# A fused attention and neighbour kernel: batch 0's distances in float32r parts, 45 unread products ahead, last rows in two banks, another order

## Chip, cores and metric

The kernel runs on one core of a Trainium2 chip. The metric is the device time of one execution in microseconds (us), the median over runs. Lower is better. Engines are named as in the profile: PE is the matrix engine (PEld its weight loads), DVE the vector engine, ACT the scalar engine, POOL the general engine, SP the engine that issues DMAs.

## What is computed

Four stages on x of shape 4 x 256 x 512 (batch, rows, features), with a context of 64 x 512 per batch:

```
# stage 0: a mixture of 8 low-rank updates
w   = softmax(x @ router_W.T + router_b)              # 8 weights per row
a   = x @ sum_over_batches(ctx).T                     # 64 values per row
x   = nan_to_num(x + 0.5 * sum_n w_n * (a @ lora_B[n].T))
# stage 1: attention of 32 heads of 16 over the 64 context rows, with a mask
q, k, v = x @ Wq.T + bq, ctx @ Wk.T + bk, ctx @ Wv.T + bv
x   = layernorm(x + (softmax(mask(q k / 4)) v) @ Wo.T + bo) * ln_g + ln_b
# stages 2 and 3 (the same twice): 4 blocks each over the 8 nearest of 512 points
d2  = sq[:, None] + sq[None, :] - 2 * ctx.T @ ctx     # ctx[b]: 512 points in 64 dimensions
idx = top 8 of -d2                                    # per point, same for both stages
for i in range(4):
    p = leaky_relu(x)
    x = (W[i] @ p + sum over 8 neighbours of W[i] @ p[:, idx]) / 9 + x
```

The points lie in the feature axis: 512 points, each with 64 context rows as coordinates. The matrix W[i] is 256 x 256 and the same for the centre and the neighbours, so that a block is one product with W[i] and one with a 0/1 matrix of 512 x 512 (`nbr`), which has a one for the point itself and for its 8 nearest.

## The kernel before

**How the order comes about.** The program doesn't write its instructions in the order of execution. Each step is handed to a planner (`Plan.add`) with its engine, an assumed cost, what it reads and writes, and for some steps a second engine that could do it. `Plan.emit` then walks over modelled time: of all steps that are ready it takes, per engine, the one with the least rank among those that could start first, and emits it. Rank is the batch's due time (`DEADLINES`, line 32, one number per batch) less the length of the longest chain behind the step. `RATES` (line 46) are assumed DMA rates, `LAG` what a DMA transpose takes to land. Engines execute their queue in the emitted order, so the assumed costs decide the order but not the durations.

**Loads.** All loads are issued by SP in the order of the lines 300 to 324, over eight lanes: `load_points(b)` is batch b's context as 64 x 512 (`raw`), `ctxT` the transposed context of all batches, `load_k(o)` a quarter of WkT, `load_xT`, `load_x`, `load_w` the rest. Batch 0's context goes to a tile of its own, `cxx0`, twice: once to the partitions 0 to 63 and once to 64 to 127.

**Start.** DVE sets `ones`; PE then makes `WARM` = 20 products of 128 x 128 from it whose result nobody reads (line 333). `lora_a` sums the context over batches into `rw`. `keys` makes kT from ctxT and WkT (line 720), and ACT or DVE copy it out with bias into `kbd` (lines 736, 748).

**Per batch.** `mixture(b)`: routing products (line 421), the softmax of the 8 weights, `z` (line 449), its transpose (`turn`, line 467 on PE for batches 0 and 1, a DMA transpose for 2 and 3), the update products (line 523, with lora_BT). `values` (line 780), `queries` (line 818), `attention` (lines 848, 859, 945, 965), layer norm. `nearest(b)`: distances, then the best 8 of each row (lines 646, 649), a 0/1 matrix `near` (656, 665), a DMA transpose (675), and a copy into `nbr` (689). `block(b, i)`, i = 0 to 7: `wp` = W[i] p (line 1021), split into an upper float32r part and the rest (lines 1034, 1037), then the product of both with `nbr` (line 1052) and the update of x (line 1068).

**Distances.** The nearest need exact products. For batches 1 to 3, `scores(b)` splits the context into its float32r value and the rest: `chl` holds value and rest above each other in 128 partitions, `clh` the rest and the value, `csq` the squares in the same two parts. Three float32r products of 128 rows make one bank of 128 x 512 distances (lines 627, 628, 629). The splits take four ACT steps of 64 x 512 (lines 607 to 610) and three POOL steps (line 615). For batch 0, `scores_first` makes the cross product as float32 from `cxx0` instead, 64 rows deep, two banks at a time in the two halves of the array (line 585), and adds the squares with one float32r product per bank (line 598).

**End.** The last batch's last block ends with `last`: the second half of the neighbour sum for rows 128 to 255 is made in two column halves of 256 (line 1090), both in the bank that holds the first half of the sum; each half has its own update (line 1107) and its own store (line 1116).

Of the kernel before, what the change touches and what calls it, by code (L numbers as in the profile page):

```python
# [8 lines left out]
F32 = mybir.dt.float32  # L9
BF16 = mybir.dt.bfloat16  # L10
F32R = mybir.dt.float32r
# [20 lines left out]
DEADLINES = (0.0, 35.0, 60.0, 67.0)  # L32
# [9 lines left out]
WARM = 20  # L42
# [22 lines left out]
class Plan:  # L65
# [39 lines left out]
    def emit(self, deadline):  # L105
# [16 lines left out]
        while ready:  # L122
# [45 lines left out]
            op.end += op.lag  # L168
# [13 lines left out]
def xattn_seq_kernel(ctx: ExitStack, tc: tile.TileContext, a: dict, out: bass.AP):  # L182
# [23 lines left out]
    def make(kind, place, name):  # L206
# [15 lines left out]


    csq0 = keep.tile([128, H], F32R, name="csq0")
    cxx0 = keep.tile([128, H], F32, name="cxx0")
    chl = {b: keep.tile([128, H], F32R, name=f"chl{b}") for b in range(1, B)}
    clh = {b: keep.tile([128, H], F32R, name=f"clh{b}") for b in range(1, B)}
# [5 lines left out]
        ["csq0", "cxx0", "chl1", "clh1"],  # L233
# [60 lines left out]
    def load_points(b):  # L294
        if b:
            load(raw[b], 0.13, lambda: raw[b].tile[0:64], a["ctx"][b])
        else:
            load("cxx", 0.13, lambda: cxx0[0:64], a["ctx"][0])

    load_points(0)  # L300
    load("cxx2", 0.13, lambda: cxx0[64:128], a["ctx"][0])
    load("small", 0.05, lambda: consts, a["small"])
    load("ctxT", 0.5, lambda: ctxT.rearrange("p c b v -> p (c b v)"), a["ctxT"])
    load_k(0)
    load_k(2)
# [3 lines left out]
    load_k(3)  # L309
    load_w("lora_BT")  # L310
    load_points(3)
    load_points(2)
    load_x(0)
    load_w("WvT")
    load_x(1)
    load("rows1", 0.5, lambda: rows1, a["rows1"].partition_broadcast(128))
# [3 lines left out]
    load_xT(1)  # L320
    load_xT(2)
# [9 lines left out]
        2.2,  # L331
# [176 lines left out]
    def mix(b, l, zb):  # L508
# [44 lines left out]
        act(0.63, lambda: A_.activation(odd.tile, v, AF.Identity, bias=zero, scale=0.0), (key, "zero"), (odd,))  # L553
# [14 lines left out]
    def scores_first(b, dist):  # L568

        sq = Buf("half", "sq0")  # L570
        act(0.6, lambda: A_.activation(sq.tile[0:64], cxx0[0:64], AF.Square), ("cxx",), (sq,))
        act(0.6, lambda: A_.copy(csq0[0:64], sq.tile[0:64]), (sq,), ("csq",))
        dve(
            0.69,
            lambda: V_.tensor_tensor(csq0[64:128], sq.tile[0:64], csq0[0:64].bitcast(F32), ALU.subtract),
            (sq, "csq"),
            ("csq2",),
            port=True,
        )
        for k in range(2):  # L580

            def cross(k=k):
                for j in (2 * k, 2 * k + 1):
                    r = slice(64 * (j % 2), 64 * (j % 2) + 64)
                    T_.matmul(
                        dist[j].tile,
                        lhsT=cxx0[r, bass.ts(j, 128)],
                        rhs=cxx0[r],
                        start=True,
                        stop=False,  # L590
                        tile_position=(64 * (j % 2), 0),
                    )

            pe(2.1, cross, ("cxx", "cxx2"), (dist[2 * k], dist[2 * k + 1], ("d2", b, 4 + k)))
            for j in (2 * k, 2 * k + 1):
                pe(
                    0.36,
                    lambda j=j: T_.matmul(dist[j].tile, lhsT=mhalf_r, rhs=csq0, start=False, stop=True),
                    ("csq", "csq2", "mhalf_r"),
                    (dist[j], ("d2", b, j)),  # L600
                )

    def scores(b, dist):
# [8 lines left out]
        def rest(out_, whole, upper, ins, key):  # L612
            pool(
                1.3,
                lambda: G_.tensor_tensor(out_(), whole.tile[0:64], upper().bitcast(F32), ALU.subtract),
                (whole, *ins),
                (key,),
            )
# [19 lines left out]
    def nearest(b):  # L638
# [46 lines left out]
        for k in range(H // 128):  # L685
# [10 lines left out]
            if b > 1:  # L696
                gone = [("d2", i, j) for i in (2 * b - 4, 2 * b - 3) for j in range(4 if i else 6)]
# [488 lines left out]
```

## Time and profile before

| | |
|---|---|
| median of 3 runs | 385.94 us (385.63 to 387.9) |
| the profiled execution | 386.5 us, its span 384.8 us |
| PE, PEld busy | 378.7, 291.5 us |
| DVE, ACT, POOL busy | 240.0, 191.3, 110.3 us |
| costliest lines on PE | L1021 120.1 us, L1052 110.3 and 99.6 us |
| loads | 25.46 MB moved by the hardware queue, HBM read 12.87 MB |

The span is the time from the first to the last instruction of the program in the profiled execution; the execution's own time has 1.7 us around it. Matrix products are pipelined: the duration of one includes its latency, so consecutive ones overlap in the profile, and what counts in a stream is the distance from start to start. A number after a line or group such as "x16" is how many instructions of the kind are merged in it; a float32 product counts twice. What stands in brackets is the idle time of the engine ahead of it and what ended it.

### The profile page before, as it was taken

The page shows a single profiled execution, that of the slowest core. Times are in us where ns is not written, and L with a number is a line of the kernel's source. Part 1 is how long each engine was busy: PE and PEld are TensorE (multiplying, and loading weights), DVE is VectorE, ACT ScalarE, POOL GpSimd, SP SyncE. Part 2 cuts the span into 40 slices and gives each one's busy share as a digit, 9 for nine tenths or more (in the row PEclk, how much of TensorE's full clock was granted, in tenths as well). Part 3 has the DMA queues.
Part 4 walks back from the last instruction along what each step waited for, and adds up shares of the span by engine and source line. Part 5 has one row for each costly group of instructions (what it writes and reads, how often), then busy time and mean ns, then how long its engine had stood idle before and what let it go on. Part 6 is the DMA issues. An engine that isn't in the chain of part 4 may idle for free.

```text
span 384.8 us, 5507 instructions
## 1 busy us (share of the span) xinstructions
PE 378.7 (98%) x2120; PEld 291.5 (76%) x2120; DVE 240.0 (62%) x445; ACT 191.3 (50%) x296; POOL 110.3 (29%) x122
## 2 busy tenths in 40 slices
PE   8999999999999999999999999999999999999996
PEld 5848747668887666887867767888888888888885
DVE  1779599995992876955966726535435435435433
ACT  2672755759688769775757722322222221222220
POOL 5483307676356426542054430400000000000000
PEclk9999999999999999999999999999999999999999
DMA  6999500162155305215014610000000001000002
GB/s 201 343 407 348 112 15 1 29 136 42 28 111 112 68 0 110 56 20 90 3 27 89 103 55 2 0 0 2 1 0 2 1 0 56 0 0 2 0 0 111
DMA packets 47386, 25.81 MB, mean 67 GB/s; under 512 B 43200, under 2 KB 43584, under 8 KB 46720
## 3 DMA queue, kind: packets, MB, share of 16 engines
q1 hardware_dynamic: 47360, 25.46, 26.6%
q8 instruction: 17, 0.28, 0.3%
q14 instruction: 9, 0.07, 0.1%
HBM read 12.87 MB, written 2.10 MB: 39 GB/s over the span
## 4 chain that ended last, share of the span: by engine, by line
PE 84%; DVE 9%; DMA 2%; SPq 2%; ACT 2%; issue 1%; DVEq 0%
PE blk L1052 31%; PE wp L1021 29%; PE q L818 7%; PE o L965 5%; PE upd L523 4%; DMA raw<-in_ctx 2%; SPq L273 2%; PE avT L945 2%; PE v L780 1%; PE route L421 1%; PE s L859 1%; DVE rest L649 1%; DVE den L900 1%; DVE s L891 1%; DVE mx L885 1%; DVE top L646 1%
## 5 line engine op out<-in xcount | busy, mean ns | idle before, releaser
L1021 PE MATMUL wp<-fT,p 128*128 128x256 f32 x512 | 120.1, 380 | 0.0
L1052 PE MATMUL blk<-nbr,wph 128*128 128x512 f32 x254 | 110.3, 434 | 0.0
L1021 PEld LDWEIGHTS wp<-fT,p 128*128 128x128 f32 x512 | 96.6, 189 | 17.9 <-issue 2.5
L1052 PE MATMUL blk<-nbr,wpl 128*128 128x512 f32 x254 | 99.6, 392 | 0.0
L1068 DVE SCALAR_TENSOR_TENSOR x<-blk,x 128x512 f32<-128x512 f32 x63 | 42.9, 683 | 69.5 <-PE blk L1052 69.5
L1034 ACT CAST wph<-wp 128x512 fp32r<-128x512 f32 x64 | 37.3, 583 | 94.9 <-PE wp L1021 94.6
L1037 DVE TENSOR_TENSOR wpl<-wp,wph 128x512 fp32r<-128x512 f32 x64 | 43.8, 685 | 37.7 <-ACT wph L1034 37.7
L1052 PEld LDWEIGHTS blk<-nbr,wph 128*128 128x128 f32 x254 | 47.8, 188 | 11.8 <-issue 1.1
L1052 PEld LDWEIGHTS blk<-nbr,wpl 128*128 128x128 f32 x254 | 47.8, 188 | 10.2 <-DVE wpl L1037 0.5
L922 POOL TENSOR_TENSOR s<-s,rden 128x512 f32<-128x512 f32 x32 | 32.6, 1052 | 53.4 <-DVE rden L912 53.4
L1004 ACT ACTIVATE p<-x 128x512 f32<-128x512 f32 x38 | 24.0, 630 | 30.4 <-DVE x L1068 26.6
L477 ACT COPY pT_a<-s 128x1024 uint16<-128x1024 uint16 x24 | 24.6, 1044 | 10.8 <-POOL s L922 6.5
L965 PE MATMUL o<-WoT,avTs 128*128 128x512 f32 x64 | 29.7, 596 | 0.0
L523 PE MATMUL upd<-lora_BT,zTs 128*128 128x512 f32 x64 | 28.8, 597 | 0.8 <-ACT zTs L471 0.8
L818 PE MATMUL q<-x1T,WqT 128*128 128x256 f32 x128 | 29.1, 382 | 0.1
L818 PEld LDWEIGHTS q<-x1T,WqT 128*128 128x128 f32 x128 | 24.0, 190 | 4.0 <-ACT x1T L471 0.6
L523 PEld LDWEIGHTS upd<-lora_BT,zTs 128*128 128x128 f32 x64 | 11.9, 190 | 14.9 <-issue 13.2
L897 ACT ACTIVATE s<-s 128x512 f32<-128x512 f32 x32 | 18.6, 626 | 7.4 <-DVE s L891 7.4
L885 DVE TENSOR_REDUCE mx<-s 128x8 f32<-128x512 f32 x32 | 20.2, 679 | 2.2 <-PE s L859 2.2
L965 PEld LDWEIGHTS o<-WoT,avTs 128*128 128x128 f32 x64 | 11.9, 189 | 11.1 <-issue 10.3
L891 DVE TENSOR_TENSOR s<-s,mx 128x512 f32<-128x512 f32 x32 | 20.2, 678 | 0.0
L900 DVE TENSOR_REDUCE den<-s 128x8 f32<-128x512 f32 x32 | 20.0, 673 | 0.1
(124 smaller groups left out, 415.5 us busy)
## 6 DMA issues: line engine op xcount, KB each, us to landing
xT<-in_xT SPq DMA_DIRECT2D x4, 512.0 KB, 9.7
x<-in_x SPq DMA_DIRECT2D x4, 512.0 KB, 11.2
out<-x SPq DMA_DIRECT2D x7, 256.0 KB, 2.0
WkT<-in_WkT SPq DMA_DIRECT2D x4, 256.0 KB, 6.5
lora_BT<-in_lora_BT SPq DMA_DIRECT2D x1, 1024.0 KB, 9.4
WvT<-in_WvT SPq DMA_DIRECT2D x1, 1024.0 KB, 11.1
rows<-in_rows SPq DMA_DIRECT2D x2, 512.0 KB, 12.3
WoT<-in_WoT SPq DMA_DIRECT2D x1, 1024.0 KB, 11.7
```

The lines of the kernel that those rows point to most:

```text
L477: lambda: A_.copy(apart.tile.bitcast(U16).rearrange("p (t n) -> p t n", t=2), src().bitcast(U16).rearrange("p (n t) -> p t n", t=2),),
L523: T_.matmul(ps2.tile, lhsT=zT.tile[:, bass.ts(c, 128)], rhs=w["lora_BT"][:, c, :], start=(c == 0), stop=(c == NC - 1),)
L818: T_.matmul(ps.tile[:, 0:S], lhsT=w["WqT"][:, c, bass.ts(o, 128)], rhs=x1T[b].tile[:, c, :], start=(c == 0), stop=(c == NC - 1),)
L885: lambda mx=mx, ps=ps: V_.tensor_reduce(mx.tile[:, 0:HPC], heads(ps), AX.X, ALU.max),
L891: lambda mx=mx, ps=ps, s=s: V_.tensor_tensor(heads(s), heads(ps), mx.tile[:, 0:HPC].unsqueeze(2).to_broadcast([128, HPC, V]), ALU.subtract),
L922: lambda s=s, g=g: G_.tensor_tensor(heads(s), heads(s), rden.tile[:, bass.ts(g, HPC)].unsqueeze(2).to_broadcast([128, HPC, V]), ALU.mult,),
L965: T_.matmul(po.tile, lhsT=avT.tile[:, bass.ts(c, 128)], rhs=w["WoT"][:, c, :], start=(c == 0), stop=(c == NC - 1),)
L1021: T_.matmul(ps.tile[:, bass.ts(k, S)], lhsT=p.tile[:, c, bass.ts(2 * m2 + k, 128)], rhs=wi[:, c, :], start=(c == 0), stop=(c == NL - 1),)
L1034: act(0.59, lambda ps=ps, hi=hi: A_.copy(hi.tile, ps.tile), (ps,), (hi,))
L1037: lambda ps=ps, hi=hi, lo=lo: V_.tensor_tensor(lo.tile, ps.tile, hi.tile.bitcast(F32), ALU.subtract),
L1052: T_.matmul(pb[o].tile, lhsT=part.tile[:, bass.ds(m % 2 * S + o * 128, 128)], rhs=nbr[b, m], start=(m == 0 and k == 0), stop=(m == H // 12 ...
L1068: lambda o=o: V_.scalar_tensor_tensor(pt[:, o], pb[o].tile, 1.0 / (KNN + 1.0), pt[:, o], ALU.mult, ALU.add),
```

## The change

1. Batch 0's distances go through `scores` like those of the other batches; `scores_first`, `csq0` and `cxx0` are gone. Batch 0's context is loaded once, into `raw`, and gets `chl` and `clh` tiles of its own. Its three subtractions are done by DVE, those of the other batches still by POOL.
2. `WARM` goes from 20 to 45, its assumed cost from 2.2 to 5.0.
3. `last` makes each column half in a bank of its own, both halves of the neighbour sum in it, so that the first half of the sum is split into columns too.
4. The order of the loads changes: ctxT is issued second, the small constants after WkT's first quarter, x of batch 0 before lora_BT, WvT before the context of batches 2 and 3, rows1 after xT1.
5. The planner's numbers change: the due times, two assumed ACT costs, and the end of a DMA transpose, which is now never ahead of the last load.

```diff
-DEADLINES = (0.0, 35.0, 60.0, 67.0)
+DEADLINES = (0.0, 33.0, 58.0, 65.0)
...
-WARM = 20
+WARM = 45
...
-            op.end += op.lag
+            if op.lag:
+                op.end = max(op.end, self.landed[-1]) + op.lag
...
-    csq0 = keep.tile([128, H], F32R, name="csq0")
-    cxx0 = keep.tile([128, H], F32, name="cxx0")
-    chl = {b: keep.tile([128, H], F32R, name=f"chl{b}") for b in range(1, B)}
-    clh = {b: keep.tile([128, H], F32R, name=f"clh{b}") for b in range(1, B)}
+    chl = {b: keep.tile([128, H], F32R, name=f"chl{b}") for b in range(B)}
+    clh = {b: keep.tile([128, H], F32R, name=f"clh{b}") for b in range(B)}
...
-        ["csq0", "cxx0", "chl1", "clh1"],
+        ["chl0", "clh0", "chl1", "clh1"],
...
     load_points(0)
-    load("cxx2", 0.13, lambda: cxx0[64:128], a["ctx"][0])
-    load("small", 0.05, lambda: consts, a["small"])
     load("ctxT", 0.5, lambda: ctxT.rearrange("p c b v -> p (c b v)"), a["ctxT"])
     load_k(0)
+    load("small", 0.05, lambda: consts, a["small"])
     load_k(2)
     load_points(1)
     load_xT(0)
     load_k(1)
     load_k(3)
+    load_x(0)
     load_w("lora_BT")
+    load_w("WvT")
+    load_points(2)
     load_points(3)
-    load_points(2)
-    load_x(0)
-    load_w("WvT")
     load_x(1)
-    load("rows1", 0.5, lambda: rows1, a["rows1"].partition_broadcast(128))
     load("mask_i", 0.12, lambda: mask_i.rearrange("p b v -> p (b v)"), a["mask"].partition_broadcast(128))
     load_x(2)
     load_w("WoT")
     load_xT(1)
+    load("rows1", 0.5, lambda: rows1, a["rows1"].partition_broadcast(128))
     load_xT(2)
...
     pe(
-        2.2,
+        5.0,
...
-        act(0.63, lambda: A_.activation(odd.tile, v, AF.Identity, bias=zero, scale=0.0), (key, "zero"), (odd,))
+        act(0.72, lambda: A_.activation(odd.tile, v, AF.Identity, bias=zero, scale=0.0), (key, "zero"), (odd,))
...
-    def scores_first(b, dist):
...
         def rest(out_, whole, upper, ins, key):
-            pool(
-                1.3,
-                lambda: G_.tensor_tensor(out_(), whole.tile[0:64], upper().bitcast(F32), ALU.subtract),
+
+            (pool if b else dve)(
+                1.3 if b else 0.69,
+                lambda: (G_ if b else V_).tensor_tensor(out_(), whole.tile[0:64], upper().bitcast(F32), ALU.subtract),
...
-        (scores if b else scores_first)(b, dist)
+        scores(b, dist)
...
             act(
-                0.62,
+                0.72,
                 lambda rest=rest, near=near: A_.activation(
...
-        pb = [Buf("bank", f"blk{b}_{i}_{o}") for o in range(NL)]
+        pb = [Buf("bank", f"blk{b}_{i}_{o}") for o in range(NL - ((b, i) == (B - 1, 2 * NBLK - 1)))]
...
-                if (b, i, m2, o) == (B - 1, 2 * NBLK - 1, 1, NL - 1):
+                if (b, i, o) == (B - 1, 2 * NBLK - 1, NL - 1):
                     continue
...
-            last(b, pb, parts[1], pt)
+            last(b, pb[0], parts, pt)
...
+    def last(b, other, parts, pt):
 
         o = NL - 1
+        ends = [Buf("bank", f"end{h}") for h in range(2)]
+        for m2 in range(2):
+            for h in range(2):
+                cols = bass.ts(h, H // 2)
+                pe(
+                    0.48,
+                    lambda cols=cols, h=h, m2=m2: [
+                        T_.matmul(
+                            ends[h].tile[:, 0 : H // 2],
+                            lhsT=part.tile[:, bass.ds(m * S + o * 128, 128)],
+                            rhs=nbr[b, 2 * m2 + m][:, cols],
+                            start=(m2 == 0 and m == 0 and k == 0),
+                            stop=(m2 == 1 and m == 1 and k == 1),
+                        )
+                        for m in range(2)
+                        for k, part in enumerate(parts[m2])
+                    ],
+
+                    (*parts[m2], ("nbr", b, 2 * m2), ("nbr", b, 2 * m2 + 1), *([other] if m2 else [])),
+                    (ends[h],),
+                )
         for h in range(2):
             cols = bass.ts(h, H // 2)
             dve(
                 0.38,
-                lambda cols=cols: V_.scalar_tensor_tensor(
-                    pt[:, o, cols], pb[o].tile[:, cols], 1.0 / (KNN + 1.0), pt[:, o, cols], ALU.mult, ALU.add
+                lambda cols=cols, h=h: V_.scalar_tensor_tensor(
+                    pt[:, o, cols], ends[h].tile[:, 0 : H // 2], 1.0 / (KNN + 1.0), pt[:, o, cols], ALU.mult, ALU.add
                 ),
-                (pb[o], ("x", b, o), ("last", h)),
+                (ends[h], ("x", b, o)),
                 (("out", h),),
             )
```

More of the change, by code (lines that the diff above doesn't have):

```diff
@@ L294, in load_points @@
     def load_points(b):
[L295 to L298, printed above, removed]
+        load(raw[b], 0.13, lambda: raw[b].tile[0:64], a["ctx"][b])
     load_points(0)
-    load("cxx2", 0.13, lambda: cxx0[64:128], a["ctx"][0])
-    load("small", 0.05, lambda: consts, a["small"])
     load("ctxT", 0.5, lambda: ctxT.rearrange("p c b v -> p (c b v)"), a["ctxT"])
     load_k(0)
+    load("small", 0.05, lambda: consts, a["small"])
     load_k(2)
@@ L564, in mix @@
         pool(1.35, lambda: G_.tensor_tensor(v, v, rows["bo"], ALU.add), ("rows1",), (key,))
-    def scores_first(b, dist):
[L570 to L601, printed above, removed]
     def scores(b, dist):
@@ L696, in nearest @@
             if b > 1:
-                gone = [("d2", i, j) for i in (2 * b - 4, 2 * b - 3) for j in range(4 if i else 6)]
+                gone = [("d2", i, j) for i in (2 * b - 4, 2 * b - 3) for j in range(4)]
             act(
@@ L1080, in block @@
                 )
-    def last(b, pb, parts, pt):
+    def last(b, other, parts, pt):
         o = NL - 1
-        for h in range(2):
-            cols = bass.ts(h, H // 2)
-            pe(
-                0.52,
-                lambda cols=cols, h=h: [
-                    T_.matmul(
-                        pb[o].tile[:, cols],
-                        lhsT=part.tile[:, bass.ds(m * S + o * 128, 128)],
-                        rhs=nbr[b, 2 + m][:, cols],
-                        start=False,
-                        stop=(h == 1 and m == 1 and k == 1),
-                    )
-                    for m in range(2)
-                    for k, part in enumerate(parts)
-                ],
-                (*parts, ("nbr", b, 2), ("nbr", b, 3), *pb),
-                (("last", h),),
-            )
+        ends = [Buf("bank", f"end{h}") for h in range(2)]
[18 more added lines that the diff above has]
+                )
         for h in range(2):
```

## The prediction

> **What bounds the kernel now.** I read the busy shares first, then the chain of waits, then the matrix engine's own order of time at the two ends of the span. Shares:
>
> ```profile
> PE 378.7 (98%) x2120; PEld 291.5 (76%) x2120; DVE 240.0 (62%) x445; ACT 191.3 (50%) x296; POOL 110.3 (29%) x122
> ```
>
> PE is busy for all but 6 us of 384.8, and this is not an average over unlike stages. In the windows the middle and the end look like this (busy us of PE, PEld, DVE, ACT, POOL, then clock and DMA):
>
> ```profile
> 50.00:60.00 10.00, 10.00 (x57) 4.80 (x56) 10.00 (x18) 3.48 (x6) 0.00 (x0) 1.00 0.01 2
> 250.00:300.00 50.00, 50.00 (x225) 42.15 (x225) 22.89 (x35) 12.63 (x21) 0.00 (x0) 1.00 0.00 1
> ```
>
> So once PE has its stream it never stops: from 250 on it repeats one block per 7.16 us (each half alternates 1.73 of wp and 1.85 of blk in the chain). DVE is full too at 50 to 60, which matters for a rival below. What can change is when the stream begins, what is in it, and what follows its last product. The chain in order of time (start, us, what) shows the beginning:
>
> ```profile
> 7.99 9.51 DMA raw<-in_ctx
> 17.50 0.02 issue
> 17.52 0.78 ACT sq L609 x2
> 18.30 0.30 issue
> 18.60 0.55 ACT kbd L736
> 19.14 0.51 ACT chl L607
> 19.65 0.49 ACT zTs L471
> 20.14 0.04 issue
> 20.19 7.13 PE upd L523 x16
> ```
>
> ACT takes its work in order: it stands at the square of raw (batches 2, 3) until that load lands, and the copy of batch 0's z stands behind it, so upd begins late. PE alone, same stretch:
>
> ```profile
> 1.12 2.32 PE L333 MATMUL idle<-ones 128*128 128x128 bf16 x20 [1.12 <-DVE ones L327]
> 3.37 4.13 PE L585 MATMUL d<-cxx 64*128 64x512 f32 x8
> 7.51 1.97 PE L720 MATMUL kT<-ctxT,WkT 128*128 128x256 f32 x8
> 9.68 1.99 PE L720 MATMUL kT<-ctxT,WkT 128*128 128x256 f32 x8 [0.20 <-DMA WkT<-in_WkT]
> 11.32 0.58 PE L598 MATMUL d<-csq,mhalf_r 128*128 128x512 f32 x1
> 18.55 0.40 PE L627 MATMUL d<-chl 128*128 128x512 f32 x1
> 18.78 0.39 PE L628 MATMUL d<-clh,chl 128*128 128x512 f32 x1
> 19.01 0.40 PE L629 MATMUL d<-csq,mhalf_r 128*128 128x512 f32 x1
> ```
>
> The reader is to see that batch 0's cross products (L585) fill a hole: kT can't start before its load lands at 7.38 (issue 3.16 plus the 4.2 that is the shortest WkT landing), and it starts at 7.51. And float32r products of 512 columns start 0.23 apart. The end:
>
> ```profile
> 380.07 0.69 DVE L1068 SCALAR_TENSOR_TENSOR x<-blk,x 128x512 f32<-128x512 f32 x1 [1.42 <-PE blk L1052]
> 381.02 0.75 DVE L1107 SCALAR_TENSOR_TENSOR x<-blk,x 128x256 f32<-128x256 f32 x2 [0.26 <-PE blk L1090]
> 381.47 0.83 SPq L1116 DMA_DIRECT2D out<-x  x2
> ```
>
> The first half's add waits until 381.02, after the last product of both halves (they share a bank).
>
> **The change, step by step.** The profiled execution took 386.5 (span 384.8, 1.7 around it); the median is 385.94, 0.56 less. I sum differences and apply them to both.
>
> *Start of the stream.* ctxT moves from the fourth issue (2.69) to the second (1.43), and WkT's first quarter from 3.16 to about 1.9. If landing follows issue, it lands 1.26 earlier, at 6.1; if bytes decide, 0.152 MB less ahead of it at the 201 GB/s of the first slice is 0.76 earlier, at 6.6. The 45 products: twenty take 2.32 of which the last's own latency is 0.31, so 0.106 apart; 45 of them from 1.12 are through at 5.9. They are covered by the wait for the load; without that cover the added 25 would cost 2.65. I take kT at 6.2 instead of 7.51: **-1.3** (-0.9 to -1.4).
>
> *Batch 0's distances.* The L585 products go out of the hole, worth nothing. The four L598 products go: 11.32 to 11.74, 16.79 to 17.21, and two from 18.00 to 18.55, 1.39 in all. Twelve float32r products come, 12 x 0.23 = 2.76, and now in the stream, because their inputs aren't ready earlier: raw lands at 3.29 (issue 0.80 plus about 2.5), then a copy on ACT and three subtractions on DVE of 0.68 (row of L575) end near 6.4. Each turn between kinds of product costs 0.1 to 0.2, as at 11.32 (0.42 instead of 0.23); I add one more, 0.15. Sum **+1.5** (+1.4 to +1.7).
>
> The rule that speaks against this step comes after the row: eight K=64 products took 4.13, two at a time in different row halves. The Trainium skill ("TensorEngine Tiling (Array Packing)", Overview) gives contractions up to 64 rows up to twice the speed when two share the array. By it the removed products are the cheaper form (four pairs at upd's 0.43 are 1.7, against 2.8), and the sum would still be near +1.5, since the old ones were in a hole anyway.
>
> *Waits in the head.* Between the first and second kT the start distance is 2.17, against 1.64 from there to 11.32: 0.5 of waiting on WkT. The twelve products can lie there: gone. Before upd, 19.01 to 20.19 is 0.95 beyond one product. Whether it goes depends on where the new order puts the squares of raw2 and raw3 against the copy of z; I take half. Sum **-0.9** (0 to -1.45). What is late next is PE itself: kT 4 x 1.73, route 1.74, zT 0.87, d1 0.7 and the new 2.76 make 13.0, so from 6.2 upd can't start before 19.2. lora_BT is not in the way: with x0 now ahead and one ctx load less, it lands between its old 16.4 and x0's old 19.0.
>
> *The clock.* The first products are 0.106 apart and the eight K=64 ones took 4.13 where four pairs at upd's 0.43 are 1.7: the array ran at half speed until near 7, though the granted clock reads 1.00 in that window. If kT starts at 6.2, its first 0.6 us run slow: **+0.3** (0 to +0.5). The skill ("TensorE: Matmul & The Clock Gate", Part 1) says that full speed comes after one busy window of about 3.4 us which runs freely. By it the speed-up may come as early as 4.5; the 45 products would end near 5.2, the load would still set kT's start, and this term would be zero.
>
> *Last rows.* Halves in two banks: same products, 16 of 256 columns at 0.12 instead of 4 of 512 and 8 of 256. The first half's add can follow L1068 at 380.8 instead of 381.02, and the last add and its store move up by about the same: **-0.25** (0 to -0.3). SP issues the same three stores.
>
> *At nothing.* One more ACT copy pair and two more DVE subtractions (1.4) at 3.3 to 6.4, where DVE waits 4.12 for kT and ACT 5.77 for raw; if that cover is gone, 1.4 in DVE's full stretch. rows1 moves behind x2, WoT and xT1: it would land near 31 instead of 25.05; vbd's add (33.02) and L564 (33.43) wait on it, and vbd's reader avT is at 67.8. The model's new rule for transposes, new costs, deadlines: no instruction is added, only the order moves. Batch 0's transposes already land after the loads (39.89, last load 39.25) and nothing needs their result until blk at 98.89.
>
> *The order after 20.* PE's stalls there beyond the fixed 0.1 to 0.2 at turns are four of 0.2 to 0.4 (at 60.0, 82.0, 122.3, 233.6), together about 1. So at most -1; I take 0.
>
> Sum: -1.3 + 1.5 - 0.9 + 0.3 - 0.25 = -0.65. The profiled execution would be 385.85, the median **385.3**. Own bounds: all best -1.4 + 1.4 - 1.45 - 0.3 - 1 = -2.75, so 383.2; all worst -0.9 + 1.7 + 0.5 = +1.3, so 387.2.
>
> **Rivals.**
>
> *Slower, through ACT's queue.* raw2 and raw3 move behind x0 and WvT. WvT lands at 21.53 now; they would land near 21.5 instead of 17.5. If the copy of z stays behind their squares, as now, it follows at 21.5 + 1.18 + 0.55 + 0.51 = 23.7, upd at 24.2 instead of 19.7: 4.5, less up to 2.1 of d1's other products that PE could put in (9 x 0.23). That is +2.4 to +4.5 on the forecast, 387.7 to 389.8. It decides as soon as one square of raw2 stands ahead of that copy. For it: this wait is on the chain now. Against it: the rates written in the planner (0.22 to 0.44 MB/us) are near what the loads show (WvT 1.05 MB in 2.5), so it should see the late landing.
>
> *Slower, through DVE.* At 50 to 70 DVE is as full as PE, and PE lives on work kept for that stretch (20 upd products at 51.74). An order that spends that work earlier leaves PE waiting for scores: each block half that is late costs 3.6; one is +3.6, 388.9. For it: deadlines are two us earlier. Against it: the amount of non-block work is unchanged, and the stream there has stalls of 0.4 at most.
>
> *Faster by over 1%.* It needs -3.9, more than all best cases together (-2.75). It would take products that run faster or fewer of them, and none are dropped.
>
> *It doesn't do what it says:* the twelve products stay late or kT still begins at 7.4 because the landing doesn't move: 386.5.
>
> **How the numbers follow.** Forecast with its bounds 0.66; landing unmoved 0.08; ACT's queue 0.12; DVE's order 0.10; over 1% faster 0.04. 1% (3.9 us) is about what a measurement of this kernel can tell from no change: under 382.1 faster, over 389.8 slower. ACT's upper end and longer or repeated DVE stalls pass it: 0.16 slower, 0.05 faster, 0.79 same. The range reaches from the best own bound to the first ends of the slower rivals: 383.2 to 388.8.
>
> **What would show it.** Right: kT's first product between 6.0 and 6.7, upd's first at 19.2 to 20.2, twelve float32r products before it, the last two adds about 0.25 nearer to the last product, and PE full from 20 to the end. Wrong: a hole before upd with ACT's square of raw as releaser, holes of over 1 us on PE between 40 and 100, or kT products at half speed past 8 us.

## The result, and the profile after

The kernel after takes 390.02 us (median of 11 runs, 388.92 to 390.94), the kernel before beside it 386.56: ratio 1.0087, 95% interval 1.0072 to 1.0103. It is 3.5 us slower by the medians (3.4 by the ratio), where 0.65 faster was forecast. Its profiled execution took 389.96 (span 388.3, before 384.8: 3.5 more). Line numbers from here on are those of the kernel after; kernels whose order is written out have others.

Busy shares of the kernel after:

```profile
PE 378.1 (97%) x2149; PEld 293.0 (75%) x2149; DVE 245.4 (63%) x445; ACT 188.4 (49%) x294; POOL 114.1 (29%) x126
```

PE works no longer than before, so the time must be idle. The windows (busy us of PE, PEld, DVE, ACT, POOL; clock, DMA share, GB/s) say where:

```profile
50.00:60.00 10.00, 10.00 (x58) 4.99 (x57) 10.00 (x18) 4.80 (x8) 0.00 (x0) 1.00 0.01 2
78.00:103.00 25.00, 21.64 (x128) 16.38 (x127) 19.97 (x38) 18.24 (x30) 13.57 (x14) 1.00 0.41 72
250.00:300.00 50.00, 50.00 (x225) 42.16 (x224) 22.87 (x35) 12.00 (x20) 0.00 (x0) 1.00 0.00 1
```

The same window of the kernel before, which the prediction didn't look at:

```profile
78.00:103.00 25.00, 24.86 (x171) 19.88 (x173) 19.93 (x44) 18.86 (x33) 12.42 (x12) 1.00 0.40 80
```

PE loses 24.86 - 21.64 = 3.22 us between 78 and 103, and nothing at 50 to 60 or from 250 on. The waits of PE from 44 to 130 in the kernel after are three (us, times, longest):

```profile
PE x1T L460 <- DVE x L547: 1.2, 1, 1.2
PE wp L980 <- DVE p L969: 1.0, 1, 1.0
PE blk L1011 <- DVE rest L608: 1.0, 1, 1.0
```

They end at 83.06, 95.27 and 100.82. I call them holes 1, 2 and 3; measured from start to start they are 1.4, 1.2 and 1.3. DVE is the releaser each time, though it is busy for only 19.97 of these 25 us, so it must itself have waited. For hole 1, the timeline of ACT in the kernel after (start, us, engine, line, what; in brackets the idle time ahead and its releaser):

```profile
76.50 0.62 ACT L648 CAST nbr<-turned 128x512 fp32r<-128x512 bf16 x1 [1.34 <-DMA turned<-near]
...
79.24 1.28 ACT L940 ACT_TABLE_LOAD   x1
80.54 0.29 ACT L940 ACTIVATE mv<-mv,eps 128x1 f32<-128x1 f32 x1
```

ACT stood 1.34 us for a DMA transpose of `near` (issued 71.95, landed 76.42) and worked without a stop from there to the square root of batch 0's layer norm, in front of which it loads a table for 1.28 us. DVE stood 2.04 us for that root; behind its reciprocal comes the masked copy L547 that x1T needs. For the other two, pieces of the chain of work that ended last (start, us, what):

```profile
82.36 0.64 DVE x L547
...
90.40 1.68 DVE hi L544
...
92.79 1.23 DVE z L442
94.05 1.04 ACT zT_a L470
...
95.12 4.35 DMA zT_t<-zT_a
```

Hole 2: the steps L537, L538 and L544 of DVE took 1.5 to 1.75 instead of 0.4 to 0.7 while POOL ran its own elementwise steps, and the leaky ReLU `p` (L969), which the next `wp` reads, stands behind them. Hole 3: DVE stood 1.94 us for the transpose of zT, which landed 4.35 us after its issue, with `rest`, the split `wpl` and so `blk` behind it. `rest` reads nothing of zT: by the program both take their tiles from the same six `half` tiles, so this is a wait for a place that the transpose still holds.

The head, PE alone:

```profile
1.12 4.04 PE L326 MATMUL idle<-ones 128*128 128x128 bf16 x45 [1.12 <-DVE ones L320]
6.22 3.69 PE L679 MATMUL kT<-ctxT,WkT 128*128 128x256 f32 x16 [1.06 <-DMA WkT<-in_WkT]
...
18.64 7.03 PE L516 MATMUL upd<-lora_BT,zTs 128*128 128x512 f32 x16
...
27.84 1.98 PE L414 MATMUL route<-rw,xT 128*128 128x72 f32 x16 [0.29 <-DMA xT<-in_xT]
30.37 0.86 PE L414 MATMUL route<-rw,xT 128*128 128x72 f32 x6 [0.55 <-DMA xT<-in_xT]
```

upd starts 1.55 earlier than before (18.64 for 20.19). Then PE waits for xT of batches 1 and 2 (landed 27.70 and 30.23), and the first score product starts at 43.70 for 43.96, with a group of three distance products of batch 1 (0.7 to 0.8) still to do that the kernel before has behind it (it made them ahead of upd). Up to there the kernel is 0.5 worse, not 1.55 better. The end on DVE:

```profile
383.63 0.69 DVE L1027 SCALAR_TENSOR_TENSOR x<-blk,x 128x512 f32<-128x512 f32 x1 [1.43 <-PE blk L1011]
384.24 0.77 DVE L1069 SCALAR_TENSOR_TENSOR x<-end,x 128x256 f32<-128x256 f32 x2
```

The adds of the two halves no longer wait for PE. From the start of PE's last product (384.27) to the end of the last add it is 0.74, before 1.07: 0.33 gained. Together 0.5 + 3.2 - 0.3 = 3.4, against 3.5 between the spans.

### The profile page after: what moved, and what is told of

It is laid out like the page before. It is cut to its first block, busy times and chain, and to the rows that moved or that the text cites. A ratio compares the mean times of both kernels' runs of the same rounds, so it can differ in the third digit from the quotient of the medians.

```text
span 388.3 us, 5585 instructions
## 1 busy us (share of the span) xinstructions
PE 378.1 (97%) x2149; PEld 293.0 (75%) x2149; DVE 245.4 (63%) x445; ACT 188.4 (49%) x294; POOL 114.1 (29%) x126
## 4 chain that ended last, share of the span: by engine, by line
PE 73%; DVE 7%; DMA 1%; ACT 1%; issue 1%; DVEq 0%; ACTq 0%
PE blk L1011 30%; PE wp L980 28%; PE o L924 5%; PE q L777 4%; DVE rest L608 2%; PE upd L516 2%; PE avT L904 2%; PE s L818 1%; DMA zT_t<-zT_a 1%; DVE lo L538 1%; DVE top L605 1%; DVE hi L544 1%; DVE hi L537 1%; PE v L739 0%; PE s L807 0%
## 5 line engine op out<-in xcount | busy, mean ns | idle before, releaser
L993 ACT CAST wph<-wp 128x512 fp32r<-128x512 f32 x64 | 37.4, 586 | 98.1 <-PE wp L980 97.8
L963 ACT ACTIVATE p<-x 128x512 f32<-128x512 f32 x40 | 24.9, 629 | 29.0 <-DVE x L1027 24.6
L488 POOL COPY pTs<-pT_t 128x1024 uint16<-128x1024 uint16 x14 | 16.3, 1169 | 21.2 <-DMA pT_t<-pT_a 14.0
```

The source lines that it names most:

```text
L963: lambda l=l: A_.activation(p.tile[:, l], pt[:, l], AF.Prelu, alpha=SLOPE),
L993: act(0.59, lambda ps=ps, hi=hi: A_.copy(hi.tile, ps.tile), (ps,), (hi,))
```

## The experiments

The median of the kernel before lay at 386.28 to 386.65 in the four groups of runs. Where an order is changed, the order that the planner emitted is written out and steps are moved in it.

### Order or work

Two kernels cross the halves. The first has the work of the kernel after in the emitted order of the kernel before from the first score products on; the second the reverse.

```diff
-order of the planner
+work of after, from the first scores on in the order of before   (work_after_order_before)
+work of before, from the first scores on in the order of after   (work_before_order_after)
```

> The changed kernel's instructions; from batch 0's first scores (43.7 us) on, every engine takes them in the order of the kernel before; the head and the last block keep their new order. Theory 'order': the three holes of PE at 81, 94 and 100 us (1.4 + 1.2 + 1.3) are gone, because the order behind 43 us makes them. The head alone is worth little by its trace (scores start 0.26 earlier, but one group of distances, 0.8, is still to do), the end -0.25: 386.0 to 387.4. Rival 'work': the loss comes from what was added (float32r products, three more subtractions, the products in two banks), whatever the order: 389 to 391.

> The kernel before; from batch 0's first scores on, every engine takes its steps in the changed kernel's order; head and last block as before. Theory 'order': holes of PE of some 3 to 4 us in all come up between 75 and 105 us: 389 to 391. Rival 'work': 386.0 to 387.2, as before.

Measured 388.76, ratio 1.0056 [1.0035, 1.0077], and 388.56, ratio 1.0055 [1.0037, 1.0072]: between the theories, both times. Neither separates them, for two reasons that show only in the traces. Each has a wait of 1.1 us before the last block (at 376.3 and 373.7) that neither parent has, since the last rows of one kernel meet the order of the other. And the first has none of holes 1 to 3 but has others (0.7 at 84, for ACT's copy of x1T; twice 0.7 at 28 and 30, for xT), the second keeps hole 2 (1.09) and has 0.25 left of hole 1.

### Three DVE steps moved

In the order of the kernel after, three steps go forward or back by a few places: the copy that hole 1 waits for goes ahead of the reciprocal that waits for ACT; `p`, which hole 2 waits for, ahead of a mixture step of batch 3; `rest`, which waits for the transpose in hole 3, behind two splits `wpl`.

```diff
-reciprocal mv (L941), copy x of batch 1 (L547)
+copy x of batch 1 (L547), reciprocal mv (L941)
-z of batch 3 (L442), p of batch 0 (L969)
+p of batch 0 (L969), z of batch 3 (L442)
-rest of batch 3 (L608), wpl (L996), wpl (L996)
+wpl (L996), wpl (L996), rest of batch 3 (L608)
```

> The changed kernel with three moves in DVE's order alone: the masked copy of x (batch 1, rows 128 to 255) ahead of the reciprocal that waits for ACT's square root; p of batch 0 ahead of z of batch 3; the two wpl of batch 0's first block ahead of a match-replace that waits for a DMA transpose. Theory 'order': each hole goes or shrinks to 0.3; 386.2 to 387.5. Rival: DVE as a whole is short of time in this stretch, and the holes come back later: 389 to 390.

Measured 387.08, ratio 1.0011 [0.9996, 1.0025]: 2.9 of the 3.4 us are back without any change of work. PE's waits from 44 to 130 in it:

```profile
PE blk L1073 <- DVE wpl L1058: 0.9, 1, 0.9
PE upd L578 <- ACT zTs L550: 0.4, 1, 0.4
```

Hole 1 is gone; from start to start, 1.2 and 0.5 are left at 96 and 101. In the profiles 2.6 us of the gain lie behind the first score product. Another 0.5 lie ahead of it (43.20 for 43.70), where xT1 landed earlier (26.88 for 27.70); the moves don't touch that. A fourth move, PE's `v` of batch 1 ahead of the routing of batches 1 and 2, was to fill the wait for xT.

```diff
-route of batch 1 (L414), route of batch 2 (L414), v of batch 1 (L739)
+v of batch 1 (L739), route of batch 1 (L414), route of batch 2 (L414)
```

> As the three moves, and on PE the values of batch 1 ahead of the routing products of batches 1 and 2, which stand for the loads of xT (holes of 0.45 and 0.7 at 27.3 and 29.5 us). Theory 'order': 0.8 to 1.1 less than with three moves, 385.2 to 386.6, so a little under the kernel before. Rival: the wait moves to q, whose weights land at 32.75, or PE's gain is eaten by DVE: the same as with three moves.

Measured 387.81, ratio 1.0024 [1.0008, 1.0039], 0.7 worse than three. The rival named the right place, q, but not the reason, and the time isn't the same but longer. In these two profiles PE has no wait for xT (it landed at 26.88 and 27.00), so there was nothing to fill. With `v` gone from between x1T and q, q stands 0.7 for ACT's copy of x1T, which `v` had covered. And an instruction fetch (see below) falls at 95.05 into zT's transpose, which lands after 4.38 instead of 3.03; the hole in front of upd at 101 grows from 0.5 to 1.0. With three moves, two of ACT's splits of wp ahead of its x1T copies, and rows1's load behind xT2:

```diff
-ACT: copies of x of batch 2 (L470), wph (L993), wph (L993)
+ACT: wph (L993), wph (L993), copies of x of batch 2 (L470)
-SP: xT1, rows1, xT2
+SP: xT1, xT2, rows1
```

> The changed kernel with the three moves of DVE, and: on ACT the two copies wph of batch 0's first block ahead of the copies that feed batch 2's DMA transposes; among the loads rows1 behind xT of batch 2. Theory 'order': of the holes that three moves left (1.2 at 96 and the waits for xT), 0.8 to 1.5 goes: 385.6 to 386.3, under the kernel before. Rival: the transposes, now later, hold up q of batch 2, and it stays at 387.

Measured 386.31, ratio 1.0005 [0.9993, 1.0018]: level with the kernel before, not below it. (Its profiled execution spans 384.3, that of the kernel before 384.8; the medians don't show this difference.)

### Moves one at a time

The first and the second edit of the three above, each alone.

> The kernel after with the first of the three moves alone: DVE's masked copy into x of batch 1 goes ahead of the reciprocal that waits for ACT's square root. Theory 'each hole by itself': the hole near 81 (1.4) falls to under 0.4 and the others stay at 1.2 and 1.3: 388.6 to 389.2, ratio to the kernel before 1.0055 to 1.0075. Rival 'DVE is late as a whole': DVE's 2.0 us of standing behind the square root only moves, the holes near 94 and 99.5 grow by what the first gives, total 389.6 to 390.3, ratio over 1.008.

> The kernel after with the second of the three moves alone: DVE's masked product of batch 0's block goes ahead of one batch-3 mixture step. Theory 'each hole by itself': the hole near 94 (1.2) falls to under 0.4, the others stay at 1.4 and 1.3: 388.7 to 389.3, ratio to the kernel before 1.0058 to 1.0078. Rival 'DVE is late as a whole': what stands behind the moved step comes later, the hole near 99.5 grows from 1.3 to 2.3 or more, total 389.6 to 390.3, ratio over 1.008.

The first move alone: 387.89, ratio 1.0028 [1.0015, 1.0042]. This is a shorter time than either theory allowed. In its profile hole 1 (1.4) is gone, hole 2 is 1.0 instead of 1.2, hole 3 is 1.6 instead of 1.3, and the first score product comes 0.5 earlier (43.21), with xT1 landed at 27.19; together 1.8, the difference of the spans. So what it gives beyond its own hole is in this profile an earlier load, which the move doesn't touch. DVE does run earlier, and zT's transpose is issued at 92.94 instead of 95.12, but a fetch at 94.90 falls into it, it takes 4.70, and hole 3 stays. The second alone: 391.7, ratio 1.0118 [1.0095, 1.0141], worse than the kernel after. Hole 2 is gone, but zT's transpose still lands at 99.02 (99.47 in the kernel after), and hole 3 takes what hole 2 gave. PE alone in that kernel:

```profile
100.38 0.51 PE L1073 MATMUL blk<-nbr,wph 128*128 128x512 f32 x1 [2.66 <-DVE rest L670]
100.88 0.79 PE L1073 MATMUL blk<-nbr,wpl 128*128 128x512 f32 x1
101.47 0.63 PE L1073 MATMUL blk<-nbr,wph 128*128 128x512 f32 x1
101.90 0.63 PE L1073 MATMUL blk<-nbr,wpl 128*128 128x512 f32 x1
```

Behind a wait of 2.66 the products start 0.43 apart instead of 0.23, until 104.0: the first eight take 1.4 us more than in the kernel after. So the rival "DVE is late as a whole" holds for the second move, and its price had a part that neither theory had.

### Is the head the loss?

Two kernels change only the head; the order of all else stays. The first has 20 unread products again. The second leaves out eight of batch 0's twelve distance products, so that the distances of batch 0 are other ones.

```diff
-WARM = 45
+WARM = 20
```

```diff
-                T_.matmul(dist[j].tile, lhsT=mine, rhs=chl[b], start=True, stop=False)
-                T_.matmul(dist[j].tile, lhsT=mine, rhs=clh[b], start=False, stop=False)
-                T_.matmul(dist[j].tile, lhsT=mhalf_r, rhs=csq.tile, start=False, stop=True)
+                if b:
+                    T_.matmul(dist[j].tile, lhsT=mine, rhs=chl[b], start=True, stop=False)
+                    T_.matmul(dist[j].tile, lhsT=mine, rhs=clh[b], start=False, stop=False)
+                T_.matmul(dist[j].tile, lhsT=mhalf_r, rhs=csq.tile, start=(b == 0), stop=True)
```

> The changed kernel with 20 unread products instead of 45; the order of all other steps is the same. PE then stands idle from 3.4 to the landing of WkT near 6.1. Theory 'clock': without the other 25 the array is still at half speed when kT starts, so kT, the distances and the routing take some us longer: +1 to +3.5, 391 to 393.5. Rival 'cover': the load sets the start of kT and the array is fast by 7 us either way: 389.5 to 390.5.

> The changed kernel without eight of the twelve float32r products of batch 0's distances (only the squares are left; the distances of batch 0 are other ones), 1.84 us less on PE; the order is the same. Theory 'loads bind the head': routing of batches 1 and 2 still waits for xT (27.7 and 30.2), so that most of it is lost: 0.2 to 0.9 less, 389.1 to 389.8. Rival 'PE binds the head': all of it comes through: 388.0 to 388.4.

With 20 products 389.47, ratio 1.0083 [1.0063, 1.0103]: as the kernel after, although PE is 2.87 us later at upd. PE alone in that kernel:

```profile
6.27 6.52 PE L679 MATMUL kT<-ctxT,WkT 128*128 128x256 f32 x16 [2.83 <-DMA WkT<-in_WkT]
...
21.51 2.74 PE L516 MATMUL upd<-lora_BT,zTs 128*128 128x512 f32 x6
```

The same 16 kT records take 6.52 instead of 3.69: behind 20 products and an idle stretch of 2.83, the array runs at half rate (0.427 apart instead of 0.216) up to 12.0. So the unread products are worth 2.9 us at upd and 1.8 at the first scores (45.50 for 43.70). The time is the same in the end, but not because the head doesn't count. Holes 1 and 3 are 0.25 and 0.2 in this kernel, only hole 2 (1.2) stays, and PE wins back 2.2 us between 78 and 103:

```profile
78.00:103.00 25.00, 23.86 (x146) 17.82 (x145) 22.30 (x43) 19.40 (x31) 13.83 (x14) 1.00 0.39 73
```

A loss in front and a gain behind cancel. Why 50 instructions fewer on PE (25 products and their weight loads) made two holes vanish was not in any theory; the next section has it.

With short distances 389.25, ratio 1.0073 [1.0053, 1.0094]: 1.8 us of PE's work less in the head, the first scores 0.83 earlier (42.87), and the time 0.8 lower, with intervals that overlap. This isn't a clean test of the head either. Hole 1 is down to 0.3 and hole 3 is gone here too, with 16 instructions fewer in front, and waits of 0.5 and 0.7 stand at 110 and 220 instead. A clean one follows below.

### What makes the transposes late

The records of DMA packets point to an answer. PE's instructions are fetched in packets of 16 KB on a queue of their own, 17 in the execution, one for each 256 instructions (2149 products and as many weight loads make 4298; from 261 us on, 256 to 258 of their records lie between two packets). In the kernel after, one starts at 73.2 and one at 97.0. The window from the issue of zT's transpose to its landing there, in 40 slices of 0.109 us (DMA busy in tenths; GB/s):

```profile
DMA  0000000000179999999999999900000000999999
GB/s 0 0 0 0 0 0 0 0 0 0 24 148 219 238 202 205 224 358 191 202 146 186 128 78 49 9 7 7 12 9 9 9 9 7 193 287 292 287 162 280
...
q8 instruction: 1, 0.02, 1.4%
```

The reader is to see the nine slices (from 97.8), 1 us, in which the transposes move 7 to 12 GB/s; in front of and behind them it is mostly 150 to 350. The instruction packet starts at 97.03 and takes 0.95, so the standstill begins while it runs and ends 0.8 after it. (That it holds one of the 16 DMA engines, and the transpose then waits for that engine's share, would fit the trickle; it wasn't tried.) The same transpose with no packet in the middle of it, in one of the kernels below (after_70_products, from 93.82 to 97.01, slices of 0.080), has no such standstill:

```profile
DMA  0000000000000016999999999999997369999999
GB/s 0 0 0 0 0 0 0 0 0 0 0 0 0 0 22 125 221 221 228 209 225 193 231 199 228 189 199 189 157 222 158 71 122 218 205 215 218 218 209 196
```

A test has to move the fetches and leave the order and PE's time alone, so the number of unread products changes while their columns stay nearly the same:

```diff
-45 products of 128 columns
+20 products of 288 columns   (after_wide_products: 50 instructions fewer, fetches later)
+70 products of 82 columns    (after_70_products: 50 instructions more, fetches earlier)
```

> The kernel after, with 20 unread products of 288 columns in place of 45 of 128: nearly the same time on PE in the head, but 50 instructions fewer on PE ahead of everything else, so that PE's instruction fetches (one for each 256 of its instructions) come some 3 us later against the work. Head as in the kernel after (kT at 6.2, first scores at 43.7 to 44.1). Theory 'fetch' (a fetch that falls into a DMA transpose makes it land 1.2 to 2 us late, and that makes the holes at 81 and 99.5): the transpose issued near 72 lands 2.4 to 2.6 after its issue in place of 4.47, the one near 95 in 3.0 to 3.4 in place of 4.35; the hole near 81 falls from 1.4 to under 0.5, the one near 99.5 from 1.3 to under 0.5, the one near 94 (DVE's masked product late) stays at 1.0 to 1.4; total 387.9 to 389.0, ratio to the kernel before 1.004 to 1.0065. Rival 'order alone': the fetches shift and the holes stay, total 389.6 to 390.4. Rival 'other transposes': the two holes shrink, and a transpose further on is hit in their place, total 389 to 390 with a new hole of about 1.

> The kernel after with 70 unread products of 82 columns in place of 45 of 128: nearly the same columns in all, 50 instructions more on PE ahead of the work, so the fetches come earlier against it: from the rows of the kernel after they would fall near 69, 90 and 99 in place of 73.2, 97.0 and 100.8. Theory 'fetch': the transpose issued near 72 lands in 2.4 to 2.6 and those near 95 in 3.0 to 3.4, the holes near 81 and 99.5 fall from 1.4 and 1.3 to under 0.5, the one near 94 stays; total 387.4 to 388.6, ratio to the kernel before 1.002 to 1.0055. Rival 'order alone' (the wide products won through their earlier loads): the two holes stay, total 389.4 to 390.3. Rival 'fewer instructions are better': slower than the kernel after, over 390.3.

Wide: 387.58, ratio 1.0025 [1.0015, 1.0035]; zT's transpose lands in 3.20, the one near 72 in 2.50, holes 1 and 3 are 0.25 each, hole 2 is 1.2. Seventy: 387.48, ratio 1.0022 [1.0007, 1.0036]. PE's fetches lie at 71.6, 89.5 and 110.8 (what lies near 99 here and at 100.8 in the kernel after, which the expectation counts with them, is an 8 KB packet of a second instruction queue); the first hits the transpose in front of the one that hole 1 hangs on, which lands at 75.05 instead of 76.42. Its window:

```profile
78.00:103.00 25.00, 23.87 (x138) 18.20 (x137) 22.28 (x42) 18.36 (x28) 13.33 (x14) 1.00 0.33 64
```

2.23 of the 3.22 us are back. The wide products also had earlier loads (xT1 at 26.46, first scores at 42.94), which are part of their gain; the seventy have them nearly as late as the kernel after (27.57, first scores at 43.56) and take as long as the wide ones. From the first scores to the end of the span the kernel after takes 344.55, the wide 342.73, the seventy 342.25. So fetches later or earlier by 50 instructions win back about 2.5 of the 3.4 us by the medians, and 1.8 and 2.3 of it lie behind the first scores.

The wide products also give the clean test of the head. The kernel with 20 narrow ones (after_20_products) has the same number of instructions in the same order, and differs only in their columns. Its first scores come at 45.50 instead of 42.94, and it takes 389.47 instead of 387.58 (ratios 1.0083 and 1.0025): of 2.6 us lost in the head, 1.9 arrive at the end (2.2 by the ratios). So the head does count.

### Fetch and order together

The six moves, and the second move alone, each with 20 products of 288 columns.

```diff
-45 products of 128 columns
+20 products of 288 columns
```

> The kernel after with the six moves of the earlier run, and with 20 unread products of 288 columns in place of 45 of 128, so that the same work on PE has 50 instructions fewer ahead of it. Theory 'fetch': the transpose issued at 71.3 lands in 2.4 to 2.6 in place of 4.02, and the holes of the earlier run at 99.8 and 108.5 (0.4 and 0.5) shrink; with the order mended there is little left for it to save: 385.4 to 386.2, ratio to the kernel before 0.998 to 0.9995, just under it. Rival 'order alone': as the six moves, 386.2 to 386.9, ratio 0.9995 to 1.001. A new collision further on would give 387 or more with a hole that shows it.

> The kernel after with the second move (DVE's masked product of batch 0's block ahead of one mixture step of batch 3) and with 20 unread products of 288 columns. Alone the move cost 1.2 us or more, alone the wide products gained 2.4. Theory 'the transpose sets the end': the hole at 92 goes, but the mixture step that now comes later feeds the transposes of zT, DVE's match load waits for them, and PE loses nearly the same at 97 to 99: 387.2 to 388.3, ratio 1.0015 to 1.0045, a hole of 0.8 to 1.6 behind 96. Rival 'each hole by itself' (the move cost only because a fetch hit the transpose): the hole at 92 goes and none takes its place, 386.2 to 386.9, ratio 0.9985 to 1.0008.

Six moves with wide products: 386.5, ratio 0.9993 [0.9982, 1.0004], not to be told from six moves (1.0005) or from the kernel before: where the order is mended, the fetch has nothing left to cost. The second move with wide products: 387.77, ratio 1.0034 [1.0017, 1.0051]. Hole 2 is gone and a wait of 1.5 for `rest` stands at 98.05, behind a transpose that takes its usual 3.17. So hole 2 lies in front of the same transpose and can't be won alone; that theory was right. After the 1.5 us the products run at full rate.

The kernel before with its fetches shifted:

```diff
-20 products of 128 columns
+45 products of 57 columns   (before_45_narrow)
+70 products of 37 columns   (before_70_narrow)
```

> The kernel before with 45 unread products of 57 columns in place of 20 of 128: the same columns in all, 50 instructions more, so that its fetches come 50 PE instructions earlier: near 73.5 (between transposes, as now), 91.8 (in the last 0.2 us of a transpose of x1T issued at 88.9), 92.6 (in one of neighbours issued at 92.1) and 44.4 (in one of zT). Theory 'fetch, where PE waits for the transpose': little to pay, 386.0 to 387.2, ratio 0.9985 to 1.002; a hole over 1 only where the page shows a transpose over 3.9 with a fetch in it. Rival 'every shift of the fetches costs': 387.5 or more. Rival 'fetches do not matter': 386.2 to 386.9 with transposes at the same landings as before.

> The kernel before with 70 unread products of 37 columns in place of 20 of 128: 100 instructions more, the fetches near 70.5 (in a transpose of neighbours issued at 69.1), 90.3 (in one of x1T issued at 88.9) and 108.3 (in one of pT). Theory 'fetch': the transposes at 69.1 and 88.9 land 1.2 to 2 us later than now; what follows on PE (the next neighbour parts, x1T of the last tiles) then comes late where it has less slack than that: 386.6 to 388.4, ratio 1.000 to 1.0045, with a hole over 0.5 near 75 or 92 that is not in the kernel before. Rival 'the order before has slack for it' (no hole, the time as before): 386.1 to 386.9.

386.32, ratio 0.999 [0.9969, 1.001], and 386.25, ratio 0.9984 [0.997, 0.9998]. Transposes are hit there too (4.46 at 107.8 in the first; 4.04 at 89.1 in the second, with a hole of 0.7 behind it at 94), and the time doesn't rise. The order of the kernel before bears the hits that were tried.

### The last rows alone

```diff
-    last rows: both halves in the bank of the first half   (kernel before)
+    last rows: a bank for each half                        (before_two_banks)
```

> The kernel before with the last rows in two banks alone; the order of all else is the same. The last adds and stores should stand 0.25 to 0.35 nearer to the last product: 386.2 to 386.5 against 386.6. Rival: the stores' own time covers it: no difference.

386.09, ratio 0.9996 [0.9983, 1.0009]: 0.2 less than the kernel before beside it, too little to be told from none by this measurement. The 0.33 stands on the records of the tail alone; in this kernel's too, it is 0.74 from the start of PE's last product to the end of the last add.

## Why the prediction was wrong

**Start of the stream, -1.3.** Right: kT starts at 6.22 for 7.51, with the landing (6.09) as its releaser.

**Batch 0's distances +1.5, waits in the head -0.9, clock +0.3.** Together +0.9 from kT to upd; measured 12.42 for 12.68, -0.26. The 45 products end unseen before the load lands, as said. They are 0.107 apart up to 4.0 and 0.056 from there, and end at 5.16, as the step's second working had it (near 5.2), not at 5.9; kT's products run at full rate from the first, so the clock's term is 0. The waits on WkT and before upd are both gone, -1.45, the best bound of that term. The distances cost more than the range allowed: the twelve products take 3.23 with their turns between kinds of product (0.47, for which 0.15 was taken), the old ones took 1.39, so +1.84. And "upd can't start before 19.2" counted a group of batch 1's distances (d1, 0.7) ahead of upd, which the new order makes behind it: -0.69. The four terms make -0.3.

**"Waits in the head", as far as the first scores.** Wrong behind upd. A stream that is 1.55 us ahead at 18.6 reaches the routing of batches 1 and 2 before their xT (waits of 0.29 and 0.55 in the records, about 0.45 and 0.7 from start to start). xT1 even lands earlier than before (27.70 for 30.47); the prediction asked what is late next only as far as upd. The landing of this load differs between the profiles: 26.46 to 28.13 in the eight other kernels with this order of loads in which unread products fill the wait for WkT. In the seven of them that have the same products ahead, the first scores lie at 42.94 to 43.59. What sets the landing was not tried.

**"The order after 20 ... I take 0".** This is the step that failed: it is +3.2. The reasoning was that no instruction is added and only the order moves, in a stream whose stalls are 0.2 to 0.4. That was read from the old order and says nothing on a new one. The new order puts the DVE steps of holes 1 and 3 behind DMA transposes, in hole 1 through ACT, and the instruction count ahead of it puts a fetch into each of these two transposes. Three places moved on DVE win 2.9 back, the fetches shifted alone 2.5; they work on the same holes and don't add up. What the fetches leave, 0.9 us (ratio 1.0022 to 1.0025), I put down to hole 2 and the waits for xT; that is argued, not shown. The prediction's own sign of being wrong, holes of over 1 us on PE between 40 and 100, is what came. Which of the planner's new numbers put these steps where they are was not tried.

**Last rows, -0.25.** 0.33 by the records of the tail.

**The rivals.** "Slower, through DVE" was right in its mechanism: PE waits for DVE. Its place was wrong (78 to 103, not 50 to 70, where PE stays full) and its price, one late block half at +3.6, came near the sum of three holes for another reason. So the nearness of 388.9 to the measured 390.02 is luck. What it held against this rival, stalls of 0.4 at most, is the same reading of the old order. The planner's model holds neither the fetches nor ACT's 1.28 us (it enters the root at 0.32), and every transpose lands 3.03 after its issue in it (1.23 and 1.8), where the kernel after shows 2.4 to 4.5 between 66 and 104; an order that it makes is a new draw, even where no instruction is added. ACT's queue didn't decide: upd has no wait for z.

Open stays whether the kernel after, timed once more in one group with its variants, would keep all of its 1.0087: the ratios are each to the kernel before in the same group, and the first scores of its one profile lie 0.1 to 0.8 later than those of the seven kernels above, by the landing of a load.

## What to carry to other kernels

Where one engine is full, price a new order by the slack of what feeds it: for each step that waits for a DMA transpose, ask who stands behind it on its engine and how long the full engine can do without. Treat the position of instruction fetches as part of the order: some 50 instructions at the front shift them, and a difference of under 1% between two orders should be tried with a few such shifts before it is called a property of the order. Time won or lost at the front counts only as far as the next load or transpose on the path lets it through (1.9 of 2.6 us here), and a test of it must keep the number of instructions, or it moves the fetches as well.

## What was not expected of the hardware

**Instruction fetches delay DMA transposes.** Over the 18 profiled executions, of the transposes issued after 45 us, 81 had a 16 KB fetch begin between 0.9 us after their issue and 0.2 us before their usual landing (2.44 for `near`, 3.20 for zT, 3.05 for x1T, 3.13 for pT); 65 of them landed over 0.6 late, the median of all 81 is 1.33 late. Of 478 with no fetch near, neither of 16 KB nor of 8 KB, 95% landed within 0.18 of the usual. Why 16 were spared was not tried. The 8 KB packets of a second instruction queue go with late landings too, less often: of 41 transposes with such a one in their middle and no 16 KB fetch near, 18 landed over 0.6 late. So does a load ahead: in the kernel before, the transpose issued at 81.70, behind a load of 512 KB issued at 81.02, took 4.72 instead of 3.05. The Trainium skill ("Runtime: NRT & Kernel Launch", Instruction fetch mechanics) says that instructions come in blocks of 16 KiB, 256 each, over a DMA queue of the sequencer, and that this is mostly hidden. The count agrees (17 in this execution), and PE itself isn't seen to wait for one; the transposes are.

**Half rate after a wait.** A wait of PE of 2.66 us was followed by 3.4 us at half rate, one of 1.48 by none. At the start of the kernel with 20 products, these ran at half rate (0.107 apart), and behind them and 2.83 us of idling it stayed so for another 5.7. In the first case the granted clock agrees (0.50 from 100.68 to 104.09). In the last the view gives 1.00 for 4 to 12, but the trace's record of the clock begins only at 12.0, and the view counts a stretch without record as 1.00; there the distance between products is the sign to go by. The same holds for the 1.00 that the prediction read at the start of the kernel before, whose record begins at 7.0. The skill ("TensorE: Matmul & The Clock Gate", Part 1) puts the fall to half rate after an idle window of about 3.4 us. Here 2.66 was enough once, so its window is no safe bound for a wait.

**DVE beside POOL.** DVE's steps of L538 and L544 took 1.50 and 1.75 instead of 0.42 and 0.68 while POOL worked at its own elementwise steps.
